# A transformer block on one core: the last group of self-attention without pieces in its units' second slots, the packed reciprocals and the divisions one slot later

## The chip, the cores and the metric

The kernel runs on one core of a Trainium2 chip. The core has a matrix engine (TensorE, PE in the profile; PEld is its loading of weights), VectorE (DVE), ScalarE (ACT), GpSimd (POOL), and SyncE (SP), which here only issues DMAs. Each engine works through its own queue in order, and an instruction that has to wait for another engine or a DMA holds up all that stands behind it in its queue. The metric is the device time of one execution in microseconds.

## The reference

The block takes x (2 x 1024 x 256), one condition vector per batch entry and a context of 77 rows. Cut to what matters here:

```
h1 = adaln(x, cond, norm1_w, norm1_b)                 # x normalised before, too
q, k, v = h1 @ wq, h1 @ wk, h1 @ wv                   # 16 heads of 64
attn = softmax(q k^T / sqrt(64))                      # 1024 x 1024 for each head and batch entry
x = (attn @ v) @ wo + bo + x
x = mha(adaln(x, ...norm2), context) + x              # cross attention
x = glu_ff(adaln(x, ...norm3)) + x
x = outer x + this;  x = x + ffn(layernorm(x))        # the second feed-forward, quantised
```

The softmax subtracts the largest score of each query and divides by the sum of the exponentials, as usual. Everything is kept in float32 in the attention.

## The kernel before

**Units, slots, pieces.** Self-attention is cut into 32 units (`NU`). Unit u is one batch entry, one pair of heads and one half (512) of the queries. A unit has 4 slots (`SLOTS`), so there are 128 slots, written out one after the other by the loop at L1068; u is slot // 4 and q is slot % 4. The keys come in 8 blocks of 128, `kb`, two for each slot. In this stretch the queues of PE, VectorE, ScalarE and GpSimd follow the order in which the loop emits instructions; only SP's order is left to the scheduler.

In its slot a unit computes the scores of two key blocks for the two heads (`scores`, L430, PE) into two PSUM tiles of two banks each. There are two such tiles in all (tag "s"), so the next slot's scores need the tiles that this slot's copy and maximum have read. ScalarE copies them to SBUF (L1075), VectorE folds them into the unit's running maximum (`running_max`, L446), which for every q but 2 comes behind the exponentials of an older unit, and for q = 2 ahead of them ("late").

**From maximum to division.** In the slot q = 0 of the next unit the maximum over keys is finished (`max_turned` L451, `max_folded` L455 to L468, VectorE) and sent through DRAM to all partitions (`max_sent`: L472, L473 on SP). At q = 2 ScalarE puts it into PSUM (`max_placed`, L477). Six slots after its scores a key block gets the maximum subtracted (`shifted`, L486, VectorE; for block 5 it is L482 on GpSimd), the exponential (L489, ScalarE) and is added to the running sum (`running_sum`, L496, GpSimd). Seven slots after its scores it is multiplied with the values (`times_v`, L504, PE); at the end of a unit L520 (ScalarE) copies the result into `aT`.

The sum is inverted in a packed form, three units later. At the end of q = 0 of unit u: `summed` (L527, PE, into one of the two "s" tiles), `sums_kept` (L537, ScalarE, into `rinv`, which has a single buffer) and `sums_packed` (L541, L546, SP: out to DRAM and back as 128 x 8). At q = 1 `inverted_packed` (L549, VectorE: a reciprocal of 128 x 8) and `inverted_spread` (L552 and twice L554, SP: back to DRAM and out over the partitions, into `rinv`). At q = 2 `normalised` (L560, GpSimd) multiplies `aT` with `rinv`.

**Pieces.** Most slots end with one piece, work of PE for another unit: `project` (keys or queries of a later pair, L365), `values` (L365) or `back_to_tokens` (L365, the output projection, whose result VectorE adds at L417 in the next slot). A group is four units, two pairs of heads of one batch entry; there are eight groups. The last 20 slots (units 27 to 31) have 16 pieces for 20 places, and the tuple `places` says where they stand. Besides, `inner` and `extras` hold jobs at given slots: the cross attention's weights (L718 to L785), the second norm of batch entry 0 (its statistics from slot 80 on, its root on GpSimd at slot 88, `root_stepped` L142 to L147; ScalarE's `centred`, L154, from slot 89 on; its transposes L163 in slots 96, 100, 108, 112), additions of a bias on GpSimd (L181, in slots 107, 109, 111, 113).

**Behind slot 127** a planner with fixed costs orders the rest: the last two units, the cross attention (scores L851, output L940) and the feed-forward parts.

Of the kernel before, what the change touches and what calls it, by code (L numbers as in the profile page):

```python
# [43 lines left out]
def block_kernel(ctx: ExitStack, tc: tile.TileContext, a: dict, out: bass.AP):  # L44
# [221 lines left out]
    with ExitStack() as sa:  # L266
# [158 lines left out]
        def scores(u, kb):  # L425
            b, pair, qh = place(u)
            sc = two_banks("sc")
            for j in range(2):
                rows = slice(j * DH, (j + 1) * DH)
                nc.tensor.matmul(  # L430
                    sc[:, j * 512 : (j + 1) * 512],
                    lhsT=kTs[b, pair][rows, kb * P : (kb + 1) * P],
                    rhs=qTs[b, pair][rows, qh * 512 : (qh + 1) * 512],
                    start=True,
                    stop=True,
                )
            sT[u, kb] = p3.tile([P, 1024], FP, tag="sT", name="sT")
            return sc

        def running_max(u, kb, sc):  # L440

            if kb == 1:
                maccs[u] = p1.tile([P, 1024], FP, tag="macc", name="macc")
            if kb:
                old = sT[u, 0] if kb == 1 else maccs[u]
                nc.vector.tensor_tensor(maccs[u], old, sc, ALU.max)  # L446


        def max_turned(u):
            wides[u] = p1.tile([P, 1024], FP, tag="wide", name="wide")  # L450
            nc.vector.transpose(wides[u], maccs.pop(u))  # L451

        def max_folded(u):
            quarters = small.tile([P, 4, SQ], FP, tag="mq", name="mq")
            nc.vector.tensor_reduce(  # L455
                quarters[:, 0, :], wides[u].rearrange("p (i k) -> p i k", k=SQ), AX.X, ALU.max
            )
            for i in range(1, 4):
                nc.vector.tensor_reduce(
                    quarters[:SQ, i, :], quarters[i * SQ : (i + 1) * SQ, 0, :].unsqueeze(2),  # L460
                    AX.X, ALU.max,
                )
            col = small.tile([SQ, SQ], FP, tag="mcol", name="mcol")
            nc.vector.tensor_reduce(
                col, quarters[:SQ, :, :].rearrange("p i k -> p k i"), AX.X, ALU.max
            )
            row = small.tile([SQ, SQ], FP, tag="mrow", name="mrow")
            nc.vector.transpose(row, col)  # L468
            return row

        def max_sent(u, row):
            nc.sync.dma_start(out=md[u].rearrange("(p k) -> p k", k=SQ), in_=row)  # L472
            nc.sync.dma_start(out=wides[u], in_=md[u].partition_broadcast(P))  # L473

        def max_placed(u):
            mbs[u] = psx.tile([P, 1024], FP, tag="mb", name="mb")
            nc.scalar.copy(mbs[u], wides[u])  # L477

        def max_used(u):

            t = sT[u, POOL_KB]
            nc.gpsimd.tensor_tensor(t, t, wides[u], ALU.subtract)  # L482
# [15 lines left out]
        def times_v(u, kb):  # L498
            b, pair, qh = place(u)
            if kb == 0:  # L500
                pavs[u] = psx.tile([P, 512], FP, tag="av", name="pav")
            for j in range(2):
                at = pair % 2 * P + j * DH
                nc.tensor.matmul(  # L504
                    pavs[u][j * DH : (j + 1) * DH, :],
                    lhsT=vs[b, pair // 2][:, kb, at : at + DH],
                    rhs=sT[u, kb][:, j * 512 : (j + 1) * 512],
                    start=(kb == 0),
                    stop=(kb == TB - 1),
                )  # L510
# [5 lines left out]
        def evacuated(u):  # L516
            b, pair, qh = place(u)
            if pair % 2 == 0 and qh == 0:
                aTs[b, pair // 2] = w8.tile([P, 2, S], FP, tag="aT", name="aT")
            nc.scalar.copy(home(u), pavs.pop(u))  # L520

        def summed(u, bank=two_banks):

            tots[u] = bank("tot")
            acc = paccs.pop(u)
            for i in range(4):
                nc.tensor.matmul(  # L527
                    tots[u][i * SQ : (i + 1) * SQ, :256],
                    lhsT=ones[:, :SQ],
                    rhs=acc[:, i * 256 : (i + 1) * 256],  # L530
                    start=True,
                    stop=True,
                )

        def sums_kept(u):
            rinvs[u] = p1.tile([P, 512], FP, tag="rinv", name="rinv")
            nc.scalar.copy(rinvs[u][:, :256], tots.pop(u)[:, :256])  # L537

        def sums_packed(u):

            nc.sync.dma_start(  # L541
                out=td[u][0, :].rearrange("(i n) -> i n", n=256),
                in_=rinvs[u].rearrange("(i k) n -> i k n", k=SQ)[:, 0, :256],
            )
            few[u] = small.tile([P, 8], FP, tag="few", name="few")
            nc.sync.dma_start(out=few[u], in_=td[u][0, :].rearrange("(p i) -> p i", i=8))  # L546

        def inverted_packed(u):
            nc.vector.reciprocal(few[u], few[u])  # L549

        def inverted_spread(u):
            nc.sync.dma_start(out=td[u][1, :].rearrange("(p i) -> p i", i=8), in_=few.pop(u))  # L552
            for j in range(2):
                nc.sync.dma_start(  # L554
                    out=rinvs[u][j * DH : (j + 1) * DH, :],
                    in_=td[u][1, j * 512 : (j + 1) * 512].partition_broadcast(DH),
                )

        def normalised(u):
            nc.gpsimd.tensor_tensor(home(u), home(u), rinvs.pop(u), ALU.mult)  # L560
# [409 lines left out]
        def at_slot(held, slot, *job):  # L970
            held.setdefault(slot, []).append(job)
# [3 lines left out]
        for n in range(NG):  # L975
# [10 lines left out]
            if n + 1 < NG:  # L986
# [2 lines left out]
                at_slot(extras, at + 10, load_pair, 2 * n + 3)  # L989
                at_slot(extras, at + 18, load_wo, n + 1)  # L990

        held = [pieces.pop(s) for s in range(NS - 20, NS) if s in pieces]
        places = (0, 1, 3, 4, 5, 12, 6, 14, 8, 9, 10, 11, 16, 17, 18, 19)
        for s, piece in zip(places, held, strict=True):
            pieces[NS - 20 + s] = piece
        extras[0] = [(project, 0, 0, "k", 1, maxima_banks), (first_stats, 1, 0)]
# [63 lines left out]
        def exponentials(old):  # L1060
            for at in old:
                shifted(*at)
                exponential(*at)
                running_sum(*at)

        def settle():
            while due:
                due.pop(0)()  # L1068

        for slot in range(NS):  # L1070
            u, q = slot // SLOTS, slot % SLOTS

            new = [(u, 2 * q + i, scores(u, 2 * q + i)) for i in range(2)]
            for v, kb, sc in new:
                nc.scalar.copy(sT[v, kb], sc)  # L1075
            v, k = (slot - LAG + 1) // SLOTS, (slot - LAG + 1) % SLOTS
            old = [(v, 2 * k + i) for i in range(2)] if v >= 0 else []
            if q:
                settle()
            for job in inner.pop(slot, []):  # L1080
                job[0](*job[1:])
            if q == 2 and u:
                max_placed(u - 1)
                max_used(u - 1)

            fold = q == 0 and u
            late = q == 2
            if late:  # L1090
                for at in new:
                    running_max(*at)
            else:
                exponentials(old)
            settle()
            if fold:
                max_turned(u - 1)
            if not late:
                for at in new:
                    running_max(*at)  # L1100
            if fold:
                max_sent(u - 1, max_folded(u - 1))
            if q == 1 and u > 2:
                inverted_packed(u - 3)
                inverted_spread(u - 3)
            w, k = (slot - LAG) // SLOTS, (slot - LAG) % SLOTS
            if w >= 0:
                for i in range(2):
                    times_v(w, 2 * k + i)
                    del sT[w, 2 * k + i]  # L1110
                if k == SLOTS - 1:
                    evacuated(w)
            if q == 2 and u > 2:
                normalised(u - 3)
            for job in extras.pop(slot, []):
                job[0](*job[1:])
            if slot in pieces:
                pieces[slot][0](*pieces[slot][1:])
            if q == 0 and u > 2:
                summed(u - 3)  # L1120
                sums_kept(u - 3)
                sums_packed(u - 3)
            if late:
                exponentials(old)
# [68 lines left out]
        for t in range(0, TB, 2):  # L1193
            u = LAST - 1 + t // 4
# [737 lines left out]
```

## Time and profile before

| | us |
|---|---|
| three runs | 1169.01, 1169.64, 1170.48; median 1169.64 |
| the profiled execution | 1170.28 |
| its span (first to last instruction) | 1168.5 |
| self-attention's loop: first scores to the end of slot 127 | 18.5 to about 768 |
| one scores-pass of PE, L430: 1024 matmuls | 258.0 busy |
| sums on GpSimd, L496: 224 of 128 x 1024 | 531.9 busy |
| subtractions on VectorE, L486: 224 | 260.4 busy, 1207 ns each |
| maxima on VectorE, L446: 224 | 1217 ns each |
| divisions on GpSimd, L560: 32 | 1267 to 1298 ns each |
| packed reciprocals, L549: 32 | 183 to 205 ns each |
| VectorE waiting at L549 for the DMA of the sums | 19.9 in 23 waits, 2.3 the longest |
| GpSimd waiting at L560 for the DMA of the inverses | 13.1 in 13 waits, 2.3 the longest |

The granted clock of TensorE is 0.999 over the span. In the profile a group of instructions is named by its line, engine and tiles ("macc<-macc,sc" writes `macc` from `macc` and `sc`). "Idle before" an instruction is the time in which its engine did nothing just before it, with the one that ended the wait behind the arrow. Matmuls are pipelined, so that neighbouring ones overlap in the list, and a slot's length is best read from the start of its first scores to the start of the next slot's.

### The profile page before, as it was taken

The numbers are of one execution on the slowest core, as the hardware profiler recorded it, in microseconds if no ns is written. First come the engines' busy times: TensorE is split into PE (matmuls) and PEld (weight loads), VectorE is DVE, ScalarE is ACT, GpSimd is POOL, SyncE is SP. The second block draws the span as 40 slices with busy tenths as digits, with TensorE's granted clock in tenths as the row PEclk, the third lists the DMA queues.
The fourth block names the chain that finished last, engine by engine and source line by source line (L and its number), as shares of the span: only waits on it lengthen the run. The fifth ranks groups of instructions, "written<-read, shape, count | busy, mean of one in ns | idle before, by whom it ended". The sixth has DMA issues, their size and how long they took to land.

```text
span 1168.5 us, 16402 instructions
## 1 busy us (share of the span) xinstructions
PE 1139.9 (98%) x5812; PEld 555.7 (48%) x5812; DVE 926.2 (79%) x1324; ACT 814.8 (70%) x1017; POOL 847.3 (73%) x644
## 2 busy tenths in 40 slices
PE   8998999999999999999999999999999999999997
PEld 4332334333343343343333333355677866486685
DVE  4799789879888888988988888878767643578597
ACT  4788888888887888788889888756453231655366
POOL 5589888888888888888888999988765523423245
PEclk9999999999999999999999999999999999999999
DMA  7111212112122121221113212121201020000000
GB/s 235 37 32 42 75 59 67 56 58 83 46 62 72 52 73 45 78 65 53 53 38 103 93 38 68 47 91 33 91 1 73 1 81 19 1 19 10 10 10 28
DMA packets 65031, 64.15 MB, mean 55 GB/s; under 512 B 23675, under 2 KB 54709, under 8 KB 64309
## 3 DMA queue, kind: packets, MB, share of 16 engines
q1 hardware_dynamic: 64885, 63.10, 17.5%
q8 instruction: 45, 0.74, 0.3%
q14 instruction: 37, 0.30, 0.1%
q10 hardware_dynamic: 64, 0.02, 0.0%
HBM read 55.36 MB, written 7.73 MB: 54 GB/s over the span
## 4 chain that ended last, share of the span: by engine, by line
PE 80%; DVE 11%; ACT 5%; issue 1%; POOL 1%; DMA 1%; DVEq 0%; ACTq 0%; POOLq 0%
PE sc L430 17%; PE pav L504 16%; PE pu L1820 9%; PE pp L365 8%; PE po L940 6%; PE pv L365 4%; PE sc L851 4%; PE po L1846 4%; PE po L365 4%; DVE macc L446 4%; DVE sT L486 3%; ACT sT L1075 2%; PE tot L527 1%; ACT sT L489 1%; PE pu L1675 1%
## 5 line engine op out<-in xcount | busy, mean ns | idle before, releaser
L496 POOL TENSOR_TENSOR pacc<-pacc,sT 128x1024 f32<-128x1024 f32 x192 | 455.7, 2374 | 47.0 <-ACT sT L489 36.3
L1075 ACT COPY sT<-sc 128x1024 f32<-128x1024 f32 x256 | 247.5, 1015 | 55.4 <-PE sc L430 49.5
L446 DVE TENSOR_TENSOR macc<-macc,sc 128x1024 f32<-128x1024 f32 x192 | 233.7, 1217 | 63.6 <-ACT sT L1075 52.1
L489 ACT ACTIVATE sT<-sT 128x1024 f32<-128x1024 f32 x256 | 259.4, 1061 | 14.0 <-DVE sT L486 12.9
L430 PE MATMUL sc<-qT,kT 64*128 64x512 f32 x1024 | 258.0, 619 | 6.4 <-DVE macc L446 5.8
L486 DVE TENSOR_TENSOR sT<-sT,mb 128x1024 f32<-128x1024 f32 x224 | 260.4, 1207 | 2.5 <-ACT mb L477 2.4
L504 PE MATMUL pav<-sT,v 128*64 128x512 f32 x1024 | 248.1, 604 | 4.6 <-ACT sT L489 4.2
L430 PEld LDWEIGHTS sc<-qT,kT 64*128 64x128 f32 x1024 | 85.7, 185 | 146.1 <-DVE macc L446 62.8
L504 PEld LDWEIGHTS pav<-sT,v 128*64 128x64 f32 x1024 | 62.0, 136 | 154.5 <-issue 73.7
L1820 PE MATMUL pu<-h2T,ffw 128*128 128x512 f32 (+1 forms) x320 | 114.4, 509 | 0.0
L496 POOL TENSOR_TENSOR pacc<-sT 128x1024 f32<-128x1024 f32 x32 | 76.2, 2383 | 40.5 <-ACT sT L489 40.5
L1820 PEld LDWEIGHTS pu<-h2T,ffw 128*128 128x128 f32 x320 | 59.6, 190 | 45.4 <-issue 40.4
L482 POOL TENSOR_TENSOR sT<-sT,wide 128x1024 f32<-128x1024 f32 x32 | 76.0, 2376 | 1.7 <-DMA wide<-md 1.7
L851 PE MATMUL sc<-h1T,G 128*128 128x512 f32 x160 | 72.0, 602 | 0.0
L940 PE MATMUL po<-U,p 128*128 128x256 f32 x320 | 71.4, 380 | 0.0
L940 PEld LDWEIGHTS po<-U,p 128*128 128x128 f32 x320 | 59.9, 190 | 8.0 <-issue 0.2
L365 PE MATMUL pp<-h1T,wk 128*64 128x512 f32 x256 | 62.1, 607 | 0.9 <-ACT h1T L622 0.9
L365 PE MATMUL po<-wo,aT 128*64 128x256 f32 x512 | 61.1, 380 | 0.3 <-POOL aT L560 0.3
L365 PE MATMUL pv<-wv,h1T 128*64 128x256 f32 x512 | 60.8, 379 | 0.0
L365 PE MATMUL pp<-h1T,wq 128*64 128x512 f32 x256 | 60.5, 593 | 0.0
L1838 DVE SCALAR_TENSOR_TENSOR gT<-pu,vecT,ge 128x512 f32<-128x512 f32 (+1 forms) x40 | 25.6, 641 | 43.4 <-ACT ge L1831 38.7
L1846 PE MATMUL po<-ffw,gT 128*128 128x256 f32 x256 | 57.3, 379 | 0.0
(195 smaller groups left out, 1456.4 us busy)
## 6 DMA issues: line engine op xcount, KB each, us to landing
wide<-md SPq DMA_DIRECT2D x32, 512.0 KB
rinv<-td SPq DMA_DIRECT2D x64, 128.0 KB
ffw<-in_L_xcond_ff_w_dram SPq DMA_DIRECT2D x3, 1024.0 KB
gd<-cw SPq DMA_DIRECT2D x32, 80.0 KB
ud<-cw SPq DMA_DIRECT2D x32, 80.0 KB
U<-ud SPq DMA_DIRECT2D x2, 1280.0 KB
wk<-in_L_xcond_attn_wk_dram SPq DMA_DIRECT2D x16, 128.0 KB
wq<-in_L_xcond_attn_wq_dram SPq DMA_DIRECT2D x16, 128.0 KB
```

Source lines behind the costliest of these rows:

```text
L365: nc.tensor.matmul(dst[half, :], lhsT=lhsT[:, half], rhs=rhs, start=start, stop=stop)
L430: nc.tensor.matmul(sc[:, j * 512 : (j + 1) * 512], lhsT=kTs[b, pair][rows, kb * P : (kb + 1) * P], rhs=qTs[b, pair][rows, qh * 512 : (qh + ...
L446: nc.vector.tensor_tensor(maccs[u], old, sc, ALU.max)
L486: nc.vector.tensor_tensor(sT[u, kb], sT[u, kb], mbs[u], ALU.subtract)
L489: nc.scalar.activation(sT[u, kb], sT[u, kb], AF.Exp)
L496: nc.gpsimd.tensor_tensor(paccs[u], old, sT[u, kb], ALU.add)
L504: nc.tensor.matmul(pavs[u][j * DH : (j + 1) * DH, :], lhsT=vs[b, pair // 2][:, kb, at : at + DH], rhs=sT[u, kb][:, j * 512 : (j + 1) * 512 ...
L851: nc.tensor.matmul(sc[:, j * 512 : (j + 1) * 512], lhsT=Gs[self.b][c][:, 2 * k + j, :], rhs=hT[:, c, self.at : self.at + 512], start=(c == 0),
L940: nc.tensor.matmul(self.po[i][:, :D], lhsT=self.t[piece // 2][:, at : at + P], rhs=Us[self.b][:, piece, :], start=(piece == 0), stop=(piec ...
L1075: nc.scalar.copy(sT[v, kb], sc)
L1820: nc.tensor.matmul(pu[:, k * 512 : k * 512 + n], lhsT=ffw1[c][:, at : at + P], rhs=hT[:, c, at0 : at0 + n], start=(c == 0), stop=(c == DC ...
L1846: nc.tensor.matmul(po[:, :D], lhsT=self.gT[:, f, k * P : (k + 1) * P], rhs=ffw2[:, f, :], start=(f == 0), stop=(f == FS - 1),)
```

## The change

Three places change.

```diff
-        places = (0, 1, 3, 4, 5, 12, 6, 14, 8, 9, 10, 11, 16, 17, 18, 19)
+        places = (0, 1, 2, 3, 4, 12, 6, 14, 7, 8, 10, 11, 15, 16, 18, 19)
...
             if fold:
                 max_sent(u - 1, max_folded(u - 1))
-            if q == 1 and u > 2:
+            if late and u > 2:
                 inverted_packed(u - 3)
                 inverted_spread(u - 3)
...
                 if k == SLOTS - 1:
                     evacuated(w)
-            if q == 2 and u > 2:
+            if q == 3 and u > 2:
                 normalised(u - 3)
```

The places count from slot 108. Before, slots 110, 115, 121 and 123 have no piece; after, slots 113, 117, 121 and 125, which are the q = 1 slots of units 28 to 31. Single pieces: the four `back_to_tokens` of the sixth group stand in 108 to 111 instead of 108, 109, 111, 112; the first half of the last pair's keys in 112 instead of 113 (the other three halves stay in 114, 120, 122); the four `values` in 115, 116, 118, 119 instead of 116 to 119; the four `back_to_tokens` of the seventh group in 123, 124, 126, 127 instead of 124 to 127.

The packed reciprocal and the DMAs that spread it go from q = 1 to q = 2 (`late` is q == 2) in every unit from 3 on; on VectorE the reciprocal then stands behind the two maxima of q = 2 and ahead of the four subtractions that follow them. The division on GpSimd goes from q = 2, where it stood behind the subtraction L482 and ahead of the unit's first sum, to q = 3, behind the third sum and ahead of the fourth. The copy L537 gets a wait for GpSimd. On SP the three DMAs of L552 and L554 stand behind up to four stores of the cross attention's weights (L767 or L785) and up to three loads (L718) that they preceded. Nothing else is added or removed, and no number of the computation changes.

## The prediction

> **What bounds the kernel now.** I read the page's busy shares first, then the windows of single units, then the chain that ended last, and at the end the rows of single slots. "Slot s" is the s-th pass of the loop at L1068 (unit s//4, q = s%4).
>
> The page, part 1, and the windows of units 26 to 31 (bounds; length, then busy of PE, PEld, DVE, ACT, POOL; clock, DMA share, GB/s):
>
> ```profile
> PE 1139.9 (98%) x5812; PEld 555.7 (48%) x5812; DVE 926.2 (79%) x1324; ACT 814.8 (70%) x1017; POOL 847.3 (73%) x644
> ```
>
> ```profile
> 629.69:653.13 23.44, 23.44 (x114) 7.75 (x112) 20.01 (x23) 20.89 (x27) 20.22 (x9) 1.00 0.32 108
> 653.13:676.28 23.15, 22.00 (x126) 8.53 (x124) 20.79 (x25) 18.19 (x22) 22.57 (x11) 1.00 0.12 41
> 676.28:699.68 23.40, 21.64 (x110) 7.44 (x108) 20.65 (x24) 18.57 (x22) 22.38 (x11) 1.00 0.14 46
> 699.68:722.77 23.09, 22.87 (x136) 9.33 (x136) 20.18 (x23) 19.31 (x24) 20.39 (x10) 1.00 0.30 86
> 722.77:744.75 21.98, 19.86 (x90) 5.76 (x88) 19.28 (x22) 18.38 (x22) 19.72 (x10) 1.00 0.12 39
> 744.75:768.30 23.55, 23.34 (x138) 9.52 (x140) 21.84 (x26) 18.16 (x21) 20.73 (x11) 1.00 0.21 57
> ```
>
> Up to unit 26 PE has no idle time; all other engines wait for it. From unit 27 on PE idles where a slot has no piece: a full slot lasts 5.51 us (scores at 751.31, 756.82, 762.33), one without a piece 3.79 (665.31 to 669.10), and then VectorE sets the pace, as the chain of waits shows in unit 30 (start, duration):
>
> ```profile
> 733.02 1.23 DVE macc L446
> 734.30 1.15 PE sc L430 x4
> 735.53 1.02 ACT sT L1075
> 736.55 1.19 DVE macc L446
> ...
> 740.10 3.47 DVE sT L486 x3
> 743.58 1.14 DVE macc L446
> 744.81 1.23 DVE macc L446
> 746.09 1.13 PE sc L430 x4
> ```
>
> The reader sees the loop: scores, copy, maximum, four subtractions, maximum, and only then the next scores. Adding up what slots 108 to 127 last beyond their pieces: 1.67 (slot 111), 0.70 (112), 1.24 (115), 0.47 (116), 0.33 (121), 0.46 (122), 2.03 (123), 0.47 (124): 7.4 us is the most that placing can return.
>
> **Part 1, the places.** Slots without a piece were 110, 115, 121, 123; they become 113, 117, 121, 125. PE's work is the same. I carry slot starts forward by rules read off rows: (a) PE: 5.51 per full slot, 3.79 without piece, 6.08 for q = 0 with its totals (722.77 to 728.84); (b) the first maximum of a slot starts 2.29 after its scores (665.31, 667.60); (c) the next scores start 1.25 after the previous slot's first maximum (743.50, 744.75); a late second maximum adds some 0.2; (d) VectorE back to back: subtraction 1.13, pair of maxima 2.46, transpose 1.34, maximum of q = 0 1.14, fold 2.37, an addition of a piece (L417) 0.6, reciprocal 0.12 to the next.
>
> A unit whose q = 1 has no piece: from the maxima of q = 3 to those of q = 1, 2.46 + 1.13 + 1.34 + 1.14 + 2.37 + 2.26 = 10.70; then (c) and (b) 1.25 + 2.29; then 2.46 + 0.12 + 4.53 = 7.11. Together 21.35 us, against 20.9 of PE and 23.1 in unit 29 now. Starts of units 28, 29, 30, 31 and the end of slot 127 come out as 676.55, 699.21, 720.75, 742.29, 764.8; they were 676.28, 699.68, 722.77, 744.75, 767.83. Unit 28 holds a new loss of 0.4: the transposes of slot 112 wait for the addition at L417 (0.60 idle now), which follows later maxima. Unit 31 has three additions on VectorE, so it gains least: 22.5 against 23.1. Sum: **-3.0 us**. Behind slot 127 PE stays full to 807.8 and the page's chain runs mostly on PE, so I carry the gain on to the end. Bounds: none of it, if VectorE meets something that I left out, to -4.2 (that, and the 1.18 that PE waits before the totals at 808.97).
>
> **Part 2, the reciprocals.** Now VectorE stands at L549 until the sums' DMA has landed: 19.9 us in 23 units. That is hidden: in unit 29 the reciprocal starts at 713.91 and the next maximum at 714.04, which by (b) could not start before 711.75 + 2.29 = 714.04. It bites where q = 1 is short (unit 30: 736.55 instead of 735.25) and in unit 20 (498.63 instead of 497.9, about 0.3). With part 1 every unit would pay it; moved behind the maxima of q = 2 (714.29 in unit 29) it no longer waits, which the 21.35 assumes. Its 0.12 now lies between maxima and subtractions, where the loop is closed in units 3, 15 and 23: +0.4. SP: L552 and the two L554 move past at most four stores (L767, L785) and three loads (L718); the slowest landing took 7.4 us from the reciprocal (402.4 to 409.8), and the division has some 11. The maximum's own DMAs keep their order.
>
> **Part 3, the divisions.** The 1.28 us at L560 leave a place where GpSimd mostly waited anyway (1.6 us before the first sum in most units) for one between the third and fourth sum, where it is busy. All behind it in the unit comes 1.25 later. Nobody notices, except in unit 22:
>
> ```profile
> 532.14 9.75 POOL L496 TENSOR_TENSOR pacc<-pacc,sT 128x1024 f32<-128x1024 f32 x4 [0.45 <-ACT sT L489]
> 541.84 0.21 POOL L142 TENSOR_TENSOR nr<-r 128x8 f32<-128x8 f32 x1
> ...
> 545.53 0.20 POOL L147 TENSOR_SCALAR nm<-nr 128x8 f32<-128x8 f32 x1
> ...
> 545.77 0.60 ACT L154 ACTIVATE xn<-r_sb,nm,r 128x256 f32<-128x256 f32 x1 [2.31 <-POOL nm L147]
> ...
> 552.80 2.11 PE L504 MATMUL pav<-sT,v 128*64 128x512 f32 x8 [0.78 <-ACT sT L489]
> ```
>
> The norm's 14 small steps follow four sums; the division of slot 87 will now stand inside those four. ScalarE's L154 waits for the last step, the copies of scores queue behind it (546.74 instead of 545.2), then maxima, subtractions, exponentials, and PE stands 0.78 at L504. That path has no slack left: **+1.3 us** (between 0.8 and 1.3).
>
> New is also that the copy at L537 must wait for the division, since `rinv` has one buffer. The division ends 4.84 + 1.24 after the unit's second sum begins: unit 6 183.11, unit 9 253.89, unit 12 324.65, unit 29 728.92; L537 starts now at 183.16, 253.96, 324.71, 728.98. It just fits, so 0. Queued behind L537 are the copies of q = 1's scores, which come 0.72 us after it, and the second scores of q = 1 need the bank that L537 empties. In slot 13 L537 came 0.34 later than usual and the scores took 2.04 instead of 1.99, so about 0.3 is free.
>
> Against part 3 a rule could be held: the Trainium skill, "SBUF — State Buffer", on engine-side and DMA-side ports, says that GpSimd and VectorE take one port pair exclusively, for a whole instruction, when VectorE reads two SBUF inputs. In rows: four subtractions take 4.60 us while a division runs beside the last two (670.07, 672.41) and 4.61 where none does in the first three (716.50, division at 719.15); L560 has 1267 to 1298 ns throughout. So the rule's lock isn't seen here; each of these VectorE instructions has one operand in PSUM, which the rule exempts.
>
> **The sum.** -3.0 + 1.3 + 0.4 - 0.3 = -1.6 us. The profiled execution took 1170.28 (span 1168.5), 0.64 above the median, so 1168.7 for its like and **1168.0** for the median. What a measurement can tell from no change is about 0.2%, 2.3 us: faster means below 1167.3, slower above 1172.0.
>
> **The rivals.**
> - *Unit 22 pays nothing*, because ScalarE or PE makes the time up: 1169.64 - 3.0 + 0.1 = 1166.7; with the wait at 808.97 gone too, 1165.5. For it: that wait's size is GpSimd's. Against it: no slack in the rows of unit 22.
> - *The gain doesn't come*, since VectorE holds 20.2 us of work per unit wherever the slots lie, and the change does for PE nothing but move holes: 1169.64 + 1.4 = 1171.0. For it: VectorE is 87 to 93% busy in units 27 to 31. Against: it idles 1.2, 2.3 and 2.2 at L549 in units 28 to 30.
> - *Slower: L537 becomes late.* One mechanism: GpSimd's division ends after L537's turn, ScalarE stands, the bank of the totals stays full, and PE's second scores of q = 1 wait. From 0.3 us of lateness on each further 0.1 costs 0.1 in each of the some 20 units whose margin is under 0.15. Late by 0.5 in all: 20 x 0.2 = 4.0, so 1168.0 + 4 = 1172.0; by 0.75: 1177. For it: margins of 0.05 us and a fifth semaphore on L537. Against: release to start takes 0.04 where GpSimd releases ScalarE (545.73 to 545.77).
> - *The port*: divisions block VectorE's subtractions, 29 x 1.28 = 37 us, 1207. The rows above speak against it.
>
> **How the numbers follow.** Forecast 0.44 (its own range 1166.6 to 1169.6), unit 22 free 0.22, no gain 0.15, L537 late 0.18, port 0.01. Faster than 1167.3: 0.12 of the forecast and 0.20 of the second, 0.32. Slower than 1172.0: 0.03 of the third, 0.17 of the fourth and the port, 0.21. Within: 0.47. The range reaches from 1165.2 (just under the second case's far end) to 1173.4 (L537 late by up to 0.57) and leaves out about 0.1 on each side.
>
> **What would show it.** Units 28 to 31 start near 676.6, 699.2, 720.8, 742.3 less what units before moved; no wait of VectorE at L549 in them; L154's first wait 3.5 us instead of 2.31 and PE's stop in slot 91 about 2.0 instead of 0.78; L537 never idle on GpSimd for more than 0.3. It is wrong if L537 waits for GpSimd in many units, if PE idles at slots 117, 121, 125 for over 2 us, or if the end moves otherwise than slot 127.

## The result, and the profile after

The changed kernel takes 1167.58 us (median of 20 runs, 1167.11 to 1169.29), the kernel before 1169.49 beside it (20 runs, 1168.80 to 1170.48). The ratio is 0.9985, 95% interval 0.9979 to 0.9991: 1.9 us less. The profiled execution took 1168.66 with a span of 1166.6, against 1170.28 and 1168.5; in both the first scores start 18.5 us into the span. In the profiles of the experiments below, which leave that stretch of the program alone, it lasts between 16.6 and 18.8 us, so single times differ by over 1 us for nothing in the loop. Below, "slot start" is therefore the start of a slot's first scores, counted so that slot 0 starts at 18.50.

The page, part 1, and the windows of units 26 to 31 (bounds; length, then busy of PE, PEld, DVE, ACT, POOL; clock, DMA share, GB/s):

```profile
PE 1139.2 (98%) x5804; PEld 556.0 (48%) x5812; DVE 923.6 (79%) x1324; ACT 815.2 (70%) x1017; POOL 845.9 (73%) x644
```

```profile
630.81:654.25 23.44, 23.44 (x114) 7.75 (x112) 19.91 (x23) 20.89 (x27) 20.16 (x9) 1.00 0.30 95
654.25:677.62 23.37, 23.29 (x142) 9.77 (x140) 20.97 (x25) 18.35 (x22) 22.62 (x12) 1.00 0.18 65
677.62:700.45 22.83, 22.01 (x108) 7.38 (x108) 20.97 (x24) 19.04 (x23) 22.52 (x11) 1.00 0.16 48
700.45:722.13 21.68, 21.23 (x122) 8.20 (x120) 19.84 (x23) 18.70 (x23) 20.16 (x10) 1.00 0.23 69
722.13:743.79 21.66, 21.21 (x106) 7.05 (x104) 19.82 (x23) 18.80 (x23) 20.15 (x9) 1.00 0.20 61
743.79:766.93 23.14, 21.72 (x126) 8.49 (x124) 21.58 (x26) 18.15 (x21) 20.93 (x10) 1.00 0.19 59
```

Busy times hardly move; lengths do. Unit 28 lasts 22.83 instead of 23.40, unit 29 21.68 instead of 23.09, unit 30 21.66 instead of 21.98. Unit 27 lost 0.22 (slot 110 has a piece now and lasts 5.51 instead of 3.78, and slot 111 gives back 1.50 of that), and unit 31 gained 0.41. But unit 26 starts later than before: 630.81 instead of 629.69. Where each microsecond went (slot starts, after less before):

| slot start | before | after | difference | what lies in between |
|---|---|---|---|---|
| 16 | 105.85 | 105.92 | +0.07 | unit 3 |
| 83 | 502.17 | 502.53 | +0.36 | 0.04 to 0.07 in each of units 7, 10, 13, 15, 19 |
| 88 | 532.00 | 532.27 | +0.27 | slot 83, 5.50 instead of 5.62; 0.07 in unit 21 |
| 92 | 556.55 | 557.94 | +1.39 | unit 22: slots 89, 90, 91 |
| 101 | 612.25 | 613.36 | +1.11 | slot 100, 6.71 instead of 7.01 |
| 112 | 676.28 | 677.62 | +1.34 | unit 27: slots 110, 111 |
| 116 | 699.68 | 700.45 | +0.77 | unit 28 |
| 120 | 722.77 | 722.13 | -0.64 | unit 29 |
| 124 | 744.75 | 743.79 | -0.96 | unit 30 |
| 127 | 762.32 | 760.93 | -1.39 | unit 31 |
| end of span | 1168.5 | 1166.6 | -1.9 | 0.2 at the start of cross attention, 0.3 in the feed-forward |

So slots 108 to 126 returned 2.5 us, and 1.1 had been lost ahead of them. Unit 22 alone lost 1.12; what the other units lost and gained up to there cancels out. The loss in unit 22, in rows of three engines that answer to those of before (start, duration, and the wait ahead with what ended it; ScalarE's copy of the scores, L1075 before, is L1076 in the changed kernel):

```profile
537.22 1.27 POOL L560 TENSOR_TENSOR aT<-aT,rinv 128x512 f32<-128x512 f32 x1
538.46 4.82 POOL L496 TENSOR_TENSOR pacc<-pacc,sT 128x1024 f32<-128x1024 f32 x2
543.24 0.21 POOL L142 TENSOR_TENSOR nr<-r 128x8 f32<-128x8 f32 x1
...
546.93 0.20 POOL L147 TENSOR_SCALAR nm<-nr 128x8 f32<-128x8 f32 x1
```

```profile
547.16 0.60 ACT L154 ACTIVATE xn<-r_sb,nm,r 128x256 f32<-128x256 f32 x1 [2.77 <-POOL nm L147]
547.67 0.56 ACT L385 COPY kT<-pp 128x512 f32<-128x512 f32 x1
548.13 1.93 ACT L1076 COPY sT<-sc 128x1024 f32<-128x1024 f32 x2
```

```profile
539.41 0.20 DVE L468 STREAM_TRANSPOSE mrow<-mcol 32x32 f32<-32x32 f32 x1
539.55 1.29 DVE L135 TENSOR_SCALAR w<-mv 128x8 f32<-128x8 f32 x1
540.87 0.17 DVE L84 TENSOR_SCALAR r<-w 128x8 int32<-128x8 int32 x1
540.95 2.35 DVE L486 TENSOR_TENSOR sT<-sT,mb 128x1024 f32<-128x1024 f32 x2
```

The division now stands inside the four sums, so the norm's 14 steps end at 547.1 instead of 545.7, L154 starts 1.39 later (0.27 of it from the slots before), and the copies of scores (548.13 instead of 546.74) and all behind them follow. PE's stop in slot 91 is 1.21 instead of 0.78. Something else is in the last rows: L135, on 8 elements a partition, lasts 1.29 us where it lasted 0.16.

The reciprocal no longer waits. Its line before, then after (durations min/median/max, first and last start), with what ended the waits of VectorE ahead of it:

```profile
L549 DVE RECIPROCAL few<-few x32: 183/203/205, 96.5 to 815.2; 128x8 f32<-128x8 f32 x32
...
  DMA few<-td: 19.9, 23
```

```profile
L549 DVE RECIPROCAL few<-few x32: 183/196/203, 100.1 to 813.6; 128x8 f32<-128x8 f32 x32
...
  DMA few<-td: 1.8, 1
```

19.9 us of waiting in 23 places became 1.8 in one, behind the loop, and the kernel is only 1.9 us faster. The experiments show how much of that waiting was hidden.

### The profile page after: what moved, and what is told of

Same layout as the page of the kernel before. It is cut to its first block, busy times and chain, and to the rows that moved or that the text cites. A ratio compares the mean times of both kernels' runs of the same rounds, so it can differ in the third digit from the quotient of the medians.

```text
span 1166.6 us, 16397 instructions
## 1 busy us (share of the span) xinstructions
PE 1139.2 (98%) x5804; PEld 556.0 (48%) x5812; DVE 923.6 (79%) x1324; ACT 815.2 (70%) x1017; POOL 845.9 (73%) x644
## 4 chain that ended last, share of the span: by engine, by line
PE 79%; DVE 10%; ACT 5%; POOL 2%; issue 2%; DMA 1%; DVEq 0%; ACTq 0%; POOLq 0%; SPq 0%
PE sc L430 17%; PE pav L504 16%; PE pu L1821 9%; PE pp L365 9%; PE po L940 6%; PE pv L365 4%; PE sc L851 4%; PE po L1847 4%; PE po L365 3%; DVE sT L486 3%; DVE macc L446 3%; ACT sT L1076 2%; POOL pacc L496 2%; ACT sT L489 1%; PE tot L527 1%
## 5 line engine op out<-in xcount | busy, mean ns | idle before, releaser
L1076 ACT COPY sT<-sc 128x1024 f32<-128x1024 f32 x256 | 247.7, 1015 | 53.7 <-PE sc L430 52.4
L482 POOL TENSOR_TENSOR sT<-sT,wide 128x1024 f32<-128x1024 f32 x32 | 76.1, 2377 | 2.0 <-DMA wide<-md 2.0
L1832 ACT ACTIVATE ge<-pu,vecT 128x512 f32<-128x512 f32 (+1 forms) x40 | 24.0, 599 | 48.3 <-PE pu L1821 48.1
```

## The experiments

Each changes the kernel before or the changed one in a few lines.

**The parts alone.** First the kernel before with the new places and nothing else:

```diff
-        places = (0, 1, 3, 4, 5, 12, 6, 14, 8, 9, 10, 11, 16, 17, 18, 19)
+        places = (0, 1, 2, 3, 4, 12, 6, 14, 7, 8, 10, 11, 15, 16, 18, 19)
```

> The places of the change alone; reciprocals and divisions stay at q = 1 and q = 2. My theory: the short q = 1 slots return 2.7 us (what the changed kernel's trace shows from slot 108 to 127), but VectorE then stands at L549 in each of them; the sums land some 7.4 us after L537, so the maxima of q = 2 come 0.4 to 1.5 us late in unit 28, 1.1 in unit 29, 1.2 in unit 30, 0.3 in unit 31, about 3.2 in all. Unit 22 pays nothing. Sum: +0.5 against before, 1170.0. Rival (the wait at L549 is hidden in the last group as it is elsewhere): -2.7, 1166.8.

Measured: 1168.32 us (11 runs, 1166.75 to 1170.66), ratio 0.9988 (0.9979 to 0.9997). Slot 116 starts 0.59, slot 120 2.00, slot 124 1.48 and slot 127 1.66 us before those of the kernel before: ahead even of the changed kernel. The theory, that every unit of the last group pays for the reciprocal's wait, is wrong; nor does the whole 2.7 us come back, as the rival had it, but 1.49 between slots 108 and 127. VectorE waits at L549 for 0.38 in unit 28, 0.42 in unit 29, not at all in unit 31, and for long only in unit 30:

```profile
728.32 2.53 DVE L446 TENSOR_TENSOR macc<-macc,sc 128x1024 f32<-128x1024 f32 x2
733.12 0.20 DVE L549 RECIPROCAL few<-few 128x8 f32<-128x8 f32 x1 [2.27 <-DMA few<-td]
733.24 2.51 DVE L446 TENSOR_TENSOR macc<-macc,sc 128x1024 f32<-128x1024 f32 x2
```

About 1.0 of such a wait VectorE has anyway, since the copies of q = 2's scores aren't there yet (1.01 ahead of the same maxima in the changed kernel, below). So 0.4 is hidden and 2.27 is not, and the lengths of unit 30 bear it out: 22.50 us here, 21.66 in the changed kernel, 0.84 lost. Unit 31 behind it, where the reciprocal doesn't wait, returns 0.18 here and 0.43 there.

Then the changed kernel with the old places, so the moved reciprocal and division alone:

```diff
-        places = (0, 1, 2, 3, 4, 12, 6, 14, 7, 8, 10, 11, 15, 16, 18, 19)
+        places = (0, 1, 3, 4, 5, 12, 6, 14, 8, 9, 10, 11, 16, 17, 18, 19)
```

> The moved reciprocals and divisions alone; places as before. My theory: unit 22 costs 1.1, the closed loops of the units with additions 0.3, units 20 and 25 return 0.4, and in unit 30, the one short q = 1 slot of the old places, the wait of 2.18 us at L549 goes and returns 1.3. Sum -0.3 against before, 1169.2; the start of slot 92 lies 1.4 later than before and that of slot 124 about 0.2 earlier. Rival (the moved division makes L537 and with it PE late in all units): slower by 2 us or more, spread evenly.

Measured: 1169.43 us (11 runs), ratio 1.0001 (0.9992 to 1.0009). Up to slot 108 it is the changed kernel to 0.01 us (+1.11), and of that unit 30 returns 0.94: slot 127 starts 0.31 late. The two parts add up: -1.66 and +0.31 make -1.35, where both together gave -1.39.

The reciprocal back at q = 1, the division late:

```diff
-            if late and u > 2:
+            if q == 1 and u > 2:
                 inverted_packed(u - 3)
```

> The changed kernel with the reciprocal and its three DMAs at q = 1 as before; the places and the later division stay. Theory: the loss of 0.35 us up to slot 83 is the reciprocal's 0.12 between maxima and subtractions and goes (slot 88 no more than 0.1 later than in the kernel before), and slot 114 lasts 5.51 instead of 5.74; unit 22's loss is the division's and stays at 1.1; in the last group the reciprocal's waits are back as with the places alone, and of them only unit 30's costs, 0.8. End of the loop 0.5 us later than in the changed kernel: some 1168. Rival: the 0.35 is the division's, so slot 88 stays 0.27 behind.

Measured: 1169.01 us in one run, beside 1170.83 for the kernel before. Slot 83 starts 0.04 us late instead of 0.36, so the small losses of units 3 to 19 are the reciprocal's. Unit 22 loses 1.10 (slot 88 +0.49, slot 92 +1.59): that loss is the division's. Unit 30 loses 1.03 against the changed kernel. Two points missed. Slot 114 lasts 5.74 here too, and in the others with the new places (but for the last one below, whose slot 113 is long), 5.50 with the old: it belongs to the places. And slot 83 lasts 6.07, where the reciprocal waits for its DMA in unit 20: 0.57 more than in the kernel with the places alone, whose reciprocal stands in the same place. It is the landing that differs between executions, and not what a wait costs: with the reciprocal at q = 1 it waits 0.88, 1.26, 1.38 and 1.83 us in unit 20 (the places alone, the move in units 28 to 31 alone, the kernel before, this one), and slot 83 lasts 5.50, 5.50, 5.62 and 6.07. The first 1.26 are hidden, and what exceeds them is lost one for one. Unit 30 does the same: waits of 2.27 and 2.46 lose 0.84 and 1.03, each the wait less 1.43.

**Where the move costs and where it pays.** The move undone in unit 21 alone, whose division meets the norm's sums in unit 22:

```diff
-            if late and u > 2:
+            moved = u != 21
+            if q == (2 if moved else 1) and u > 2:
...
-            if q == 3 and u > 2:
+            if q == (3 if moved else 2) and u > 2:
                 normalised(u - 3)
```

> The changed kernel with the reciprocal and division of unit 21's passes (the ones that stand ahead of the norm's root on GpSimd) put back to q = 1 and q = 2; all other units as changed. My theory: the 1.1 us that slots 88 to 91 last longer go, 1.1 us faster than the changed kernel, near 1166.5; L154 waits 2.3 us again and the DVE step L135 takes 0.2 instead of 1.29 us. Rival (the stop of unit 22 comes from the moved reciprocal or the later DMAs of unit 22 itself): no change against the changed kernel, 1167.6.

Measured: 1166.08 us (6 runs, 1165.51 to 1167.23), ratio 0.9971 (0.9960 to 0.9983). Slots 89 and 90 are back at 5.87 and 6.04, slot 91 at 6.54; slot 92 starts 1.18 before the changed kernel's and slot 127 1.22.

The move in units 28 to 31 alone: the same edit with `moved = u > 27`.

> The changed places, with reciprocals and divisions moved only in units 28 to 31, where q = 1 is short. My theory: the last group returns its 2.7 us and no other unit pays or gains, 1169.5 - 2.7 = 1166.8, faster than the changed kernel by about 0.8. Rival (part of the last group's return comes from VectorE or GpSimd being further ahead when it begins, because the moves apply all along): 1167.6 or more.

Measured: 1166.16 us (5 runs, 1165.49 to 1166.23), ratio 0.9968 (0.9955 to 0.9980). Slot 88 starts 0.13 before the kernel before's, slot 127 2.72. So outside the last group the move costs more than it brings. By the medians this version and the one before it beat the kernel before by 3.2 and 3.3 us and the changed one, which ran at another time, by 1.4 and 1.5; by the start of slot 127 they are 1.33 and 1.22 ahead of the changed one.

And in unit 24 besides, `moved = u == 24 or u > 27`, to find what shortened slot 100:

> The changed kernel's places, and reciprocal and division one slot later in unit 24 and in units 28 to 31 alone. In the changed kernel slot 100 lasted 6.71 instead of 7.01 us; with the step late in units 28 to 31 alone it lasted 7.01. Theory: moving unit 24's reciprocal out of slot 97 and its division out of slot 98 is what shortens slot 100, so this is 0.3 us faster than late in 28 to 31 alone (median 1166.16): 1165.9, slot 100 6.71, and no loss in units 3, 15, 21, 22, 23. Rival: it came from the moves in other units before it, and the time is 1166.2 with slot 100 at 7.01.

Measured: 1167.27 us (11 runs, 1166.46 to 1168.37), ratio 0.9977 (0.9968 to 0.9986), with slot 100 at 7.06: so far the rival holds. Its time doesn't: the median is 1.1 above that of the move in units 28 to 31 alone, of which 0.23 arise up to slot 127 (0.17 in slot 116) and the rest, by the two profiles, outside the loop. Slot 100 lasts 7.01 to 7.07 in this kernel and in each whose reciprocals stay at q = 1 in the units before it, and 6.71 where they are moved, except in the next experiment, which moves them all and has 7.07. So it isn't the move as such. In the kernel before, VectorE stands for 0.46 us between the two maxima of slot 99, ahead of slot 100, with nothing in the trace to wait for; in the changed kernel it doesn't. What sets that stays open.

**The long L135.** The same step written as a reduction, and the seed as a constant:

```diff
-            self.mv = small.tile([P, TB, 2], FP, tag="mv8", name="mv")
+            self.mv = small.tile([P, TB, 3], FP, tag="mv8", name="mv")
...
+        def root_seeded(self):
+            nc.gpsimd.memset(self.mv[:, :, 2], EPS)
+            nc.gpsimd.memset(self.r, 1.0)
+
+        def root_reduced(self, lo, n):
...
+            nc.vector.tensor_reduce(w, self.mv[:, lo : lo + n, 1:3], AX.X, ALU.add)
+            self.root_stepped(lo, n)
...
-        at_slot(extras, first + 8, lambda: norms[1, 0].root_on_pool(0, TB))
+        at_slot(extras, first + 8, lambda: norms[1, 0].root_reduced(0, TB))
```

The reduction adds the variance and a column that holds EPS. The kernel leaves out the seed L84 of this root, so the root's values differ; GpSimd's 14 steps have the same sizes and order.

> The changed kernel, but in slot 88 the norm's first VectorE step (L135, a tensor_scalar of 128x8) is a reduction over two columns, and the seed of the root (L84) is a constant written in slot 80; GpSimd's 14 steps are the same, so the time can be read (the root's values differ). In the changed kernel L135 took 1293 ns, ending 32 ns after the sum that GpSimd had begun before it; L549, a reciprocal in SBUF alone, took 183 to 203 ns beside running GpSimd operations in 32 of 32 cases. Theory: only the tensor_scalar is held up, so the reduction takes under 0.3 us, and of unit 22's loss of 1.11 us (slots 89, 90, 91: 6.09, 6.51, 6.96 against 5.87, 6.04, 6.52) that of slot 89 goes, 0.22, perhaps a part of slot 90's, while L154 still starts near 547.2 with 2.8 us of waiting on GpSimd, for the 14 steps start when GpSimd's sums end: slot 92 starts 1.0 to 1.2 us after the kernel before less the 0.27 that it was behind in slot 88, so 0.85 to 0.9 lost in unit 22. Rival: the hold-up makes most of it, and unit 22 loses 0.4 or less. Second rival: any VectorE operation is held up while GpSimd works; then the reduction takes over 1 us and nothing changes.

Measured: 1167.93 us in one run. VectorE's reduction (L145 here) lies wholly inside a sum of GpSimd (L506 here) and isn't held up:

```profile
537.08 2.35 POOL L506 TENSOR_TENSOR pacc<-pacc,sT 128x1024 f32<-128x1024 f32 x1
...
538.17 0.12 DVE L145 TENSOR_REDUCE w<-mv 128x8 f32<-128x16 f32 x1
538.21 1.20 DVE L496 TENSOR_TENSOR sT<-sT,mb 128x1024 f32<-128x1024 f32 x1
```

Slot 89 is back at 5.87, yet slot 92 starts 25.65 after slot 88, against 25.66 in the changed kernel and 24.54 before. Unit 22 loses 1.11 without the hold-up and 1.12 with it, where the theory had 0.85 to 0.9 without it; neither rival holds. What the hold-up took in slots 89 and 90 now falls in slot 91 (7.50 instead of 6.96), where ScalarE waits (L164 and L157 here are L154 and L147 of the other kernels):

```profile
545.77 0.60 ACT L164 ACTIVATE xn<-r_sb,nm,r 128x256 f32<-128x256 f32 x1 [3.42 <-POOL nm L157]
```

So the hold-up only brings part of the loss forward; the end is set by GpSimd's 14 steps.

**How near L537 is to being late.** Four small GpSimd operations ahead of each division:

```diff
             if q == 3 and u > 2:
+                pad = small.tile([P, 8], FP, tag="pad", name="pad")
+                for _ in range(4):
+                    nc.gpsimd.tensor_scalar(pad, vecT[:, :8], 1.0, 0.0, ALU.mult, ALU.add)
                 normalised(u - 3)
```

> The changed kernel with four small GpSimd operations (128x8, which write a tile that nothing reads) ahead of each division, so that it ends later by four times 0.20 to 0.28 us (the duration and the spacing of the norm's steps), 0.8 to 1.1 us. In the changed kernel the division ended at most 0.10 us after the first scores of q = 1 began, L537 began 0.18 after them and the second scores 0.96; the second scores follow L537 by 0.43 where L537 sets them (the kernel with the division one sum later), so L537 may begin 0.53 after the first scores at no cost. Theory, as the prediction's third rival had it: beyond that each 0.1 us costs 0.1 in each unit whose division ends that late (some 20 of 28): L537 0.9 to 1.2 after the first scores, second scores 0.4 to 0.7 late, 8 to 15 us, 1176 to 1183 us. Rival: the price is 1.9 for 1, as in units of the kernel with the division one sum later (3.75 us for scores 1.95 late): 1183 to 1196 us. Second rival: PE makes it up, under 1171.

Measured: 1183.82 us in one run. Unit 6, on GpSimd, ScalarE and PE (the bracket is the wait):

```profile
159.54 1.04 POOL L1117 TENSOR_SCALAR pad<-vecT 128x8 f32<-128x8 f32 x4
160.54 1.27 POOL L560 TENSOR_TENSOR aT<-aT,rinv 128x512 f32<-128x512 f32 x1
```

```profile
161.85 0.37 ACT L537 COPY rinv<-tot 128x256 f32<-128x256 f32 x1 [0.90 <-POOL aT L560]
162.12 1.02 ACT L1076 COPY sT<-sc 128x1024 f32<-128x1024 f32 x1
```

```profile
160.81 1.13 PE L430 MATMUL sc<-qT,kT 64*128 64x512 f32 x4
162.27 1.13 PE L430 MATMUL sc<-qT,kT 64*128 64x512 f32 x4 [0.33 <-ACT rinv L537]
```

Here is the chain of the third rival: division, L537, and PE's second scores, which wait for the bank. Where L537 starts 1.04 to 1.14 us after the slot's first scores, the second scores are 0.50 to 0.61 late and the slot lasts 0.60 to 0.71 longer in the units up to 26 (unit 22: 0.98). Where L537 starts at 0.54, they are on time and the slot lasts 0.1 longer. So the price is 1 for 1, as the theory had it, and 0.1 besides. That makes 11.9 us up to slot 117. In that slot, where the division comes later still, the second scores are 2.26 late, the granted clock is halved for a while (as in the next experiment), and 3.7 us are lost; the time ends just above the theory's range.

And the division later by a whole sum:

```diff
                 running_sum(*at)
+                if at == old[0] and q == 0 and u > 3:
+                    normalised(u - 4)
...
-            if q == 3 and u > 2:
+            if q == 3 and u == 31:
                 normalised(u - 3)
```

> The changed kernel with the division later by one more sum of GpSimd (2.4 us): between the first and second sum of the next unit's slot q = 0, in units 3 to 30. Theory of the prediction's third rival: L537 must then wait for the division in most units, by some 2.4 us; 0.3 of it is free, the rest is paid by PE's second scores of q = 1: 2.1 us in each of some 22 units up to unit 26, so about 46 us, near 1213 us; waits of ScalarE at L537 on GpSimd near 2.4 us each. Rival, from the changed kernel's trace, in which L537 waited up to 1.2 us on the division without any time lost on PE: more is free, 1.2 us or over, and the time is under 1195. Second rival: all of it is hidden, below 1169.

Measured: 1242.39 us in one run. L537's waits (us, times):

```profile
L537 ACT COPY rinv<-tot x32: 353/373/373, 90.3 to 882.2; 128x256 f32<-128x256 f32 x32
...
  POOL aT L560: 69.4, 28
```

2.48 us each, as the theory had it. In units 4 to 23 the second scores are 1.4 to 2.0 late and their slots last 1.5 to 3.8 longer, far more in some units than in others for the same lateness. The granted clock tells why. Units 6 and 9 have the same stop of 1.78 us ahead of the second scores, and lose 3.74 and 2.05. Their slots q = 1 as windows (the third number from the end is the granted clock), then rows of PE in unit 6 and in unit 9:

```profile
165.56:175.88 10.32, 8.54 (x44) 3.66 (x40) 5.31 (x7) 4.76 (x7) 7.33 (x5) 0.83 0.17 52
245.44:254.09 8.65, 6.87 (x53) 3.32 (x49) 5.29 (x7) 4.76 (x7) 6.57 (x4) 1.00 0.20 63
```

```profile
169.53 2.15 PE L365 MATMUL pk<-cT,cw 128*64 128x160 f32 x16
171.45 2.79 PE L504 MATMUL pav<-sT,v 128*64 128x512 f32 x8
```

```profile
249.41 1.31 PE L365 MATMUL pk<-cT,cw 128*64 128x160 f32 x16
250.54 1.89 PE L504 MATMUL pav<-sT,v 128*64 128x512 f32 x8
```

In unit 6 the clock is at 0.50 from 169.84 to 173.25, and PE's matmuls stretch; in unit 9 it stays at 1.00. The trace has 15 such stretches of 3.41 us in the loop, each behind a stop of 1.77 us or more; six stops as long, and all shorter ones (1.27 us at most), are followed by none, and what decides between them no run here shows. Where the clock holds, a slot lasts 1.54 longer for second scores 1.44 late and 2.05 for 1.95: again the lateness and 0.1. Most slots with a stretch lose about 1.7 more, half of 3.41 (1.3 in three of them), which makes an estimated 24 us of the 73 by which slot 127 starts after the changed kernel's. The other 49 are near the theory's 46, so its price was right, and what it left out is the clock (0.978 over the span). The rival that saw more room is wrong: none of these waits is free.

## Why the prediction was right, and where it was not

The forecast was 1168.0 with the sum -1.6; the median is 1167.58, and the span became 1.9 shorter. That the sum comes this near is in part luck: its four terms measure -2.5, +1.1, +0.4 and -0.1, together -1.1 us, and the other 0.8 comes from slot 100 and from behind the loop, where nothing was forecast. The starts of units 28 to 31, less the 1.11 from before, are 676.5, 699.3, 721.0 and 742.7, within 0.4 of those forecast. Of the steps:

- *The last group, -3.0:* mis-sized, it is -2.5 to slot 127. Slots 113, 117, 121 and 125 do stop PE for little (0.25 in two of them, 1.22 in slot 125), as rule (c) has it. But rule (c) gave the late second maximum "some 0.2", and the slots behind those without a piece, 118, 122 and 126, last 5.98, 5.97 and 5.98 instead of 5.51, so 0.47; slot 114 takes 0.24 more. The rows of slot 118 show it:

```profile
710.66 1.13 PE L430 MATMUL sc<-qT,kT 64*128 64x512 f32 x4 [0.25 <-DVE macc L446]
711.98 1.13 PE L430 MATMUL sc<-qT,kT 64*128 64x512 f32 x4 [0.20 <-DVE macc L446]
713.04 1.94 PE L504 MATMUL pav<-sT,v 128*64 128x512 f32 x8
```

  Eight scores in one run take 1.99; in two runs of four they take twice 1.13 and the 0.20 between. I had counted the gap, not the second start of the pipeline, though the list of the slots before had 0.46 and 0.47 behind slots without a piece. Units 29 and 30 last 21.68 and 21.66 for the forecast's 21.54: half of this error is made up for by the slots q = 1, which last 0.32 longer than PE's work and not the 0.46 that the forecast's 21.35 leaves. Units 28 and 31 miss by 0.17 each. The new loss in slot 112 is there as worked out: 7.80 instead of 7.37.
- *"With part 1 every unit would pay it":* wrong. Of the 2.5, the reciprocal's new place gives about 1.0: 0.84 in unit 30 and 0.25 in unit 31 behind it. With the places alone the waits were 0.38, 0.42, 2.27 and none, for the sums land 5.07, 5.65 and 7.52 us after L537 in units 28 to 30; the first experiment's expectation let them take 7.4 in each. The prediction read the wait at L549 rightly as hidden in unit 29, but not that the same cover, ScalarE's copies, is there in the new order too. In the changed kernel, unit 30:

```profile
731.07 2.53 DVE L446 TENSOR_TENSOR macc<-macc,sc 128x1024 f32<-128x1024 f32 x2
734.60 2.55 DVE L446 TENSOR_TENSOR macc<-macc,sc 128x1024 f32<-128x1024 f32 x2 [1.01 <-ACT sT L1076]
737.07 0.20 DVE L549 RECIPROCAL few<-few 128x8 f32<-128x8 f32 x1
```

- *Unit 22, +1.3 (0.8 to 1.3):* +1.12, and by the mechanism named: it goes when the division of slot 87 goes back. The two marks were off, L154's wait 2.77 instead of 3.5 and PE's stop in slot 91 1.21 instead of 2.0, because the held-up L135 made slots 89 and 90 late already. Without it L154 waits 3.42, and PE stops twice in slot 91, for 0.20 and 1.29, and the loss is the same. That PE had no idle time up to unit 26, as the prediction began, is not so: its own row of slot 91 has 0.78.
- *Closed loops, +0.4:* +0.36 by slot 83, and +0.04 when the reciprocal alone goes back. It falls in units 3, 7, 10, 13, 15 and 19 at 0.04 to 0.07 each; I had named 3, 15 and 23, at more, so that the size is right and the places mostly not.
- *Unit 20, -0.3:* -0.12. A reciprocal that is not moved loses there what its wait exceeds 1.26 us by: nothing, nothing, 0.12 and 0.57 in four executions. So the gain is there, but its size is the landing's spread.
- *L537, 0:* right, and narrow. In the changed kernel the division ends at most 0.10 us after the first scores of q = 1, L537 starts 0.18 to 0.25 after them instead of 0.14 in most units, and the second scores stay at 0.96. Of the "about 0.3" that was said to be free nearly all is: L537 at 0.54, 0.36 later, still lets the second scores be on time, and the slot is 0.1 longer. The 7.2 us for which ScalarE now waits on the division there were 8.4 of waiting on PE's totals in the profile before. So the sign that I had set, no wait on GpSimd over 0.3, was a poor one: six waits of 1.12 to 1.20 cost nothing, because ScalarE had stood there as long for PE.
- *The port:* the subtractions weren't held up, as the rows had shown. But "the rule's lock isn't seen here" went too far. L135 is such an instruction: the profile before had it too, three times behind the loop, at 1.48, 2.23 and 1.62 us. The Trainium skill, "SBUF — State Buffer", section "SBUF: two separate sides", names two ways in which VectorE takes the pair that it shares with GpSimd: two SBUF inputs, and a two-port performance mode. I had weighed the first alone. That L135 runs in such a mode no trace here shows; that it is held up to the end of GpSimd's operation, they do.
- *The rivals:* "unit 22 pays nothing" and "the gain doesn't come" each fail on their own rows: unit 22 loses 1.12, and slot 127 starts earlier. The median lies between their times (1166.7, 1171.0) and below every run of the kernel before; 1166.7 is so near that the slot starts, and not the median, speak against it. "L537 late" failed as a forecast, and the last two experiments show its mechanism and its price. The wait ahead of the totals behind the loop stayed at 1.18.

Not foreseen: slot 100's 0.30, and the 0.2 and 0.3 us behind the loop. From slot 127 to the end the profiles of the other kernels here differ from the kernel before by anything between -0.5 and +0.3 us, and no run here explains it.

## What to carry to other kernels

Waits that a profile lists with 19.9 us were worth about 1 us, at one place: ask at each place what the waiting engine would have waited for next. A move that is right in one stretch should be made there alone; where PE has no slack, a step of 1.3 us on an engine that seems idle cost 1.1 in the one unit that had a chain behind it, and restricting it gave more than the whole change. When a change adds a wait that just fits, measure how far it is from being late: here 0.3 us of room lay ahead of a price of 0.6 and more in each of some twenty units. And when a loss comes out larger in some repetitions than in others, look at the granted clock before naming a cause: here it took up to 1.7 us behind each of 15 stops of PE.

## What the runs showed of the hardware

A small VectorE tensor_scalar can be held up by a running GpSimd tensor_tensor until that ends. In the tail of the changed kernel, where a 128 x 1024 sum (the third of these) ends near 876.9:

```profile
872.06 7.26 POOL L917 TENSOR_TENSOR pacc<-pacc,p 128x1024 f32<-128x1024 f32 x3
...
874.66 2.24 DVE L135 TENSOR_SCALAR w<-mv 128x4 f32<-128x4 f32 x1
876.93 0.17 DVE L84 TENSOR_SCALAR r<-w 128x4 int32<-128x4 int32 x1
```

In all seven cases of the two kernels in which L135 began with more than 0.16 us of a GpSimd operation to go, it ended 24 to 32 ns after that operation (1.26 us to go: 1.29; 2.22 to go: 2.24). Otherwise it took 0.16. The reciprocal L549, as small and in SBUF alone, took 183 to 205 ns beside running GpSimd operations in 63 of 64 cases, the reduction 0.12. So the kind of VectorE's instruction counts. GpSimd's counts too, it seems: early in the kernel before, L574, a tensor_scalar of L135's size and kind, took 0.16 with 0.58 us of a GpSimd tensor_scalar (L633) still to run when it ended. The one ahead of it (L573) took 0.43 instead of 0.17 there, so the rule isn't settled by these rows.

The clock: behind 15 of 21 stops of PE of 1.77 to 2.30 us in the last experiment's loop, the granted clock was 0.50 for 3.41 us, starting 0.0 to 1.5 us after the stop, and most of these slots lost about 1.7 us by it; behind the stops of 1.27 us and less it never was.

The small DMA round trip of the sums landed 5.07, 5.65 and 7.52 us after L537 in three successive units of the kernel with the places alone, so a landing time read off one unit doesn't hold for the next.
